# Three routed mixtures in a twelve-stage network: gate logits per tile, gather order, place sums, and statistics

## Chip, cores and metric

The kernel runs on one core of a Trainium2 chip. The metric is the device time of one execution in microseconds (us). The time before is 3292.99 us, the median of three runs (3290.18 to 3300.77).

## What is computed

`x` is a state of 1024 tokens by 256 values. Twelve blocks follow one another, each a residual over a layer norm: in each of four layers a cross attention, a self attention and a feed-forward block.

```python
x = x + L0_xattn(layernorm(x), ctx, ...)
x = x + L0_attn(layernorm(x), ...)
x = x + L0_ffn(layernorm(x), Wg, W1, W2, W3)
...                                   # L1: xattn, attn, ffn (a convolution)
x = x + L2_xattn(...); x = x + L2_attn(...)
x = x + L2_ffn(layernorm(x), wg_red, wg, w1, b1, w2, b2)
x = x + L3_xattn(...); x = x + L3_attn(...)
x = x + L3_ffn(layernorm(x), router_w, w1, w2)
```

Three feed-forward blocks are mixtures of 8 experts. Written per token they are:

```python
# L0_ffn: the two best of 8 experts, softmax over those two
logits = x @ Wg.T                       # 1024 x 8
out = sum over the two of  gate * ((silu(x @ W1[e].T) * (x @ W2[e].T)) @ W3[e].T)
# L2_ffn: the best expert; logits through a 16-wide reduction and unit rows
logits = (x @ wg_red.T) @ (wg / max(norm(wg), 1e-4)).T
out = max(softmax(logits)) * (gelu(x @ w1[e] + b1[e]) @ w2[e] + b2[e])
# L3_ffn: the two best; a token past an expert's capacity of 320 is dropped for it
out = sum over the two of  gate * keep * (gelu(x @ w1[e]) @ w2[e])
```

## The kernel before

All tokens live in `x`, 8 tiles of 128 tokens on the partitions by 256 values. `xn` holds the normalised rows in the same shape. The stages run one after another, as one program; within a stage a scheduler orders each engine's instructions by data, except where a helper pins an instruction to its place in the program's text (`pinned`, and everything while `self.fixed` is set). Each engine carries out its own list in order.

**The hand-over between stages.** When an attention has the output of a tile, `finish_x(t)` (L360) adds it to `x` on VectorE (DVE) and calls `ready(t)` (L294): statistics on DVE (bn_stats L300, bn_aggr L302), three tiny operations on GpSimd (POOL, L306 to L308: epsilon, power, product), and, one call later, `normalise` (L314) on ScalarE (ACT), which writes `xn`. The next stage transposes `xn` on TensorE (PE; `tr` is L200, `mm` L196) and copies it out of PSUM (`to_T`, `evac` L186 and L188). Where a layer has an output bias, `add_bias` (L353) adds it to all 8 tiles of `x` on POOL at some time after `xn` has been read from them.

**A mixture** (L0_ffn, L2_ffn, L3_ffn) has these steps:

1. `expert_rows`: `xn` is written to DRAM as `xin` (one DMA on the SP queue), with rows of zeros behind it; `xn` is transposed.
2. `gate_logits`: per tile two matmuls against the gate's 8 columns, all into one PSUM bank; one copy `lg` (L1417). In L2_ffn a reduction to 16 (`xr`) and the unit rows `wu` stand between (from L1653).
3. `top2` or `first_max` (L1382 and after): the best one or two experts per token as one-hot rows, on DVE. In `two_choices` the one-hots and gates are copied together (L1587 to L1591).
4. `places`: a matmul by ones gives the count per group of 128 tokens and expert; `cum` is their running sum over 16 groups (8 in L2_ffn), one dependent add of 8 columns each (L1431); `place` (L1435) adds the place within the group, from a triangular matmul.
5. `slots`: each token's slot in a list of tiles of 128 rows (23, 15 and 23 tiles for the three mixtures), `rows` (which expert's weights a tile needs), and by matmuls of `R` (L1495, a 128x128 compare for each group) with `V` (L1481 to L1488) the lists `token` and `share` (to L1505).
6. `experts`: for each tile, `fetch` brings the weights `W` (two DMAs on SP, L1522; 2.36 MB in L0_ffn, 2.10 MB in L2_ffn and L3_ffn; three buffers) at the row that SP reads out of `rows`, and gathers 128 rows of `xin` by `token` into `xs` (an indirect DMA on the POOL queue, L1524). `turn` transposes `xs`, `hidden` and the second matrix run on PE, `y` (L1554) is scaled by `share` and scatter-added to DRAM (L1555). Fetches go two tiles ahead:

```python
got = [fetch(0), fetch(1)]
xT = turn(got[0][1])
for i in range(tiles):
    W, xs = got.pop(0)
    if i + 2 < tiles:
        got.append(fetch(i + 2))
    hT = hidden(W, xT)
    if i + 1 < tiles:
        xT = turn(got[0][1])
```

Afterwards `x` is loaded back (four DMAs, L1561), and after L0_ffn and L2_ffn `ready(t)` runs for the 8 tiles.

**The stages around.** L0_attn ends in a loop over tiles (transposes of `att`, four `py` matmuls, `finish_x`) with a PSUM pool `pst` of two banks in its second part. L2_attn ends in two matmuls a tile over `oT`. L3_attn ends in an MLP, whose second matrix keeps PE busy up to the end; it begins with convolutions over `a` (copies L2026 out of transposed `xn`), and `kb` (L2014) is an operation of POOL at its start. L1_xattn follows L0_ffn, L3_xattn follows L2_ffn.

Of the kernel before, what the change touches and what calls it, by code (L numbers as in the profile page):

```python
# [16 lines left out]
P = 128  # L17
B, S, D = 16, 64, 256
NT = B * S // P
NTOK = B * S  # L20
# [154 lines left out]
class Net:  # L175
    def __init__(self, tc, io):
        self.tc, self.nc, self.io = tc, tc.nc, io
        self.flip = 0
        self.fixed = False
# [36 lines left out]
    def load_constants(self, pool):  # L216
# [24 lines left out]
        self.ident = self.c("ident")  # L241
        self.due = None
# [52 lines left out]
    def ready(self, t):  # L295


        nc, x = self.nc, self.x[:, t, :]
        st = self.stat.tile([P, 6], F32, tag="bst", name="bst")
        nc.vector.bn_stats(st, x)  # L300
        mv = self.stat.tile([P, 2], F32, tag="mv", name="mv")
        nc.vector.bn_aggr(mv, st)  # L302
        self.normalise()

        rs = self.stat.tile([P, 2], F32, tag="rs", name="rs")
        nc.gpsimd.tensor_tensor(rs[:, 0:1], mv[:, 1:2], self.c("eps"), ALU.add)  # L306
        nc.gpsimd.tensor_tensor(rs[:, 0:1], rs[:, 0:1], self.c("pow")[:, 0:1], ALU.pow)  # L307
        nc.gpsimd.tensor_scalar(rs[:, 1:2], mv[:, 0:1], rs[:, 0:1], -1.0, ALU.mult, ALU.mult)  # L308
        self.due = t, rs

# [39 lines left out]
    def add_bias(self, i):  # L350

        for t in range(NT):
            self.nc.gpsimd.tensor_tensor(self.x[:, t, :], self.x[:, t, :], self.bv(i), ALU.add)  # L353
# [225 lines left out]
    def L1_xattn(self, w):  # L579
# [8 lines left out]
        with (  # L588
# [4 lines left out]
            with (  # L593
                tc.tile_pool(name="l1xn", bufs=1) as wn,
                tc.tile_pool(name="l1xn_t", bufs=4, space=PSUM) as pst,
            ):
                xnT = self.norm_T(wn, pst, "pst")
                self.add_bias(2)
                for c in range(4):
                    for h in range(2):  # L600
                        ps = self.psum(pst, [P, 512], "pst")
                        tok = slice(h * 512, (h + 1) * 512)
                        self.project_T(ps, Wq, xnT, slice(c * P, (c + 1) * P), tok)
                        self.evac(qT[:, c, tok], ps)
            with (
# [123 lines left out]
                def at(t, fn, *args):  # L729
                    extra.setdefault(t, []).append((fn, args))  # L730

# [300 lines left out]
    def L0_attn(self, w):  # L1032
# [4 lines left out]
        with (  # L1037
# [78 lines left out]
            with (  # L1116
# [6 lines left out]
                state = {}  # L1123

# [196 lines left out]
    def L2_attn(self, w):  # L1321
        nc, tc = self.nc, self.tc
        Wq, Wk, Wv, Wfc = w
        with (
# [4 lines left out]
        ):  # L1329
            xnT = self.norm_T(wk, pst, "pst")  # L1330
# [46 lines left out]
    def first_max(self, small, lg, tag):  # L1377
# [3 lines left out]
        m = small.tile([P, NT, 1], F32, tag=f"m{tag}", name=f"m{tag}")  # L1381
        nc.vector.tensor_reduce(m, lg, AX.X, ALU.max)  # L1382
        oh = small.tile(shape, F32, tag=f"oh{tag}", name=f"oh{tag}")
# [5 lines left out]
        lo = small.tile([P, NT, 1], F32, tag=f"lo{tag}", name=f"lo{tag}")  # L1389
        nc.vector.tensor_reduce(lo, oh, AX.X, ALU.min)  # L1390
        nc.vector.tensor_tensor(oh, oh, lo.to_broadcast(shape), ALU.is_equal)
        return m, oh

    def top2(self, small, lg):

        nc = self.nc
        shape = [P, NT, E]
        m1, oh1 = self.first_max(small, lg, "a")
        lg2 = small.tile(shape, F32, tag="lg2", name="lg2")
        nc.vector.scalar_tensor_tensor(lg2, oh1, -BIG, lg, ALU.mult, ALU.add)  # L1400
        m2, oh2 = self.first_max(small, lg2, "b")
        e2 = small.tile([P, NT, 1], F32, tag="e2", name="e2")
        nc.vector.tensor_tensor(e2, m2, m1, ALU.subtract)
        nc.scalar.activation(e2, e2, AF.Exp)
        g1 = small.tile([P, NT, 1], F32, tag="g1", name="g1")
        nc.vector.tensor_scalar(g1, e2, 1.0, None, ALU.add)
        nc.vector.reciprocal(g1, g1)
        g2 = small.tile([P, NT, 1], F32, tag="g2", name="g2")
        nc.vector.tensor_tensor(g2, e2, g1, ALU.mult)
        return oh1, g1, oh2, g2  # L1410

    def gate_logits(self, small, pp, xT, w):
        ps = self.psum(pp, [P, NT, E], "pst")
        for t in range(NT):
            self.project_N(ps[:, t, :], xT, t, w)
        lg = small.tile([P, NT, E], F32, tag="lg", name="lg")
        self.nc.vector.tensor_copy(lg, ps)  # L1417
        return lg

    def places(self, small, pp, oh, K):  # L1420
# [3 lines left out]
        G = K * NT  # L1424
# [3 lines left out]
        cum = small.tile([P, G + 1, E], F32, tag="cum", name="cum")  # L1428
        nc.vector.memset(cum[:, 0, :], 0.0)
        for g in range(G):  # L1430
            nc.vector.tensor_tensor(cum[:, g + 1, :], cum[:, g, :], ps[:, g, :], ALU.add)  # L1431
        ps = self.psum(pp, [P, G, E], "pst")
        self.mm(ps.rearrange("p g e -> p (g e)"), self.c("tri"), flat)
        place = small.tile([P, G, E], F32, tag="place", name="place")
        nc.vector.tensor_tensor(place, ps, cum[:, :G, :], ALU.add)  # L1435
        return place, cum[:, NT, :], cum[:, G, :]

    def slots(self, small, pp, oh, gate, place, count, K, tiles):
# [54 lines left out]
        for g in range(G):  # L1493
            R = small.tile([P, P], F32, tag="R", name="R", bufs=3)
            nc.vector.tensor_scalar(R, self.c("iota128"), lo[:, g : g + 1], None, ALU.is_equal)  # L1495
            self.mm(ps, R, V[:, :, g, :], g == 0, g == G - 1)
# [11 lines left out]
    def experts(self, name, xin, slots, weights, width, cols, tiles, wp, sp, pst, pso, hidden):  # L1508
# [7 lines left out]
        def fetch(i):  # L1516
# [4 lines left out]
            for o in (slice(0, cols), slice(cols, width)):  # L1521
                nc.sync.dma_start(W[:, o], self.io[weights][bass.ds(r, P), o])  # L1522
            xs = sp.tile([P, D], F32, tag="xs", name="xs", bufs=3)
# [4 lines left out]
            return W, xs  # L1528
# [10 lines left out]
        got = [fetch(0), fetch(1)]  # L1539
        xT = turn(got[0][1])  # L1540
        for i in range(tiles):
            W, xs = got.pop(0)
            if i + 2 < tiles:
                got.append(fetch(i + 2))
            hT = hidden(W, xT)
            if i + 1 < tiles:
                xT = turn(got[0][1])
            n = hT.shape[1]
            W2 = W[:, cols : cols + n * D].rearrange("p (c n) -> p c n", n=D)
# [15 lines left out]
        if name != "l3":  # L1565
            for t in range(NT):
                self.ready(t)

    def expert_rows(self, wk, stat, pst, name):

        nc = self.nc
        xn = self.xn
        xin = self.dram.tile([NTOK + SPARE, D], F32, tag=f"{name}i", name=f"{name}i")
        nc.sync.dma_start(xin[:NTOK, :].rearrange("(t p) d -> p t d", p=P), xn)
        zero = wk.tile([P, D], F32, tag="zero", name="zero")
        nc.gpsimd.memset(zero, 0.0)
        nc.sync.dma_start(xin[NTOK:, :], zero)
        xnT = wk.tile([P, 2, NTOK], F32, tag="xnT", name="xnT")
        self.to_T(pst, "pst", xn, xnT)
        return xin, xnT  # L1580

    def two_choices(self, small, pst, oh1, g1, oh2, g2, cap=None):
# [3 lines left out]
        oh = small.tile([P, 2 * NT, E], F32, tag="oh", name="oh")  # L1586
        nc.vector.tensor_copy(oh[:, :NT, :], oh1)  # L1587
        nc.vector.tensor_copy(oh[:, NT:, :], oh2)
        gate = small.tile([P, 2 * NT], F32, tag="gate", name="gate")
        nc.vector.tensor_copy(gate[:, :NT], g1[:, :, 0])  # L1590
        nc.vector.tensor_copy(gate[:, NT:], g2[:, :, 0])  # L1591
# [14 lines left out]
    def L0_ffn(self, _):  # L1606
        nc, tc = self.nc, self.tc
        with (
# [8 lines left out]
            xin, xnT = self.expert_rows(wk, stat, pst, "l0")  # L1617
            lg = self.gate_logits(small, pst, xnT, self.gates[:, :, 0:E])
# [22 lines left out]
    def L2_ffn(self, _):  # L1641
        nc, tc = self.nc, self.tc
        shape = [P, NT, E]
        with (
# [8 lines left out]
            xin, xnT = self.expert_rows(wk, stat, pst, "l2")  # L1653

            sq = small.tile([E, 16], F32, tag="sq", name="sq")
            nc.vector.tensor_tensor(sq, self.wg2, self.wg2, ALU.mult)
            nr = small.tile([E, 1], F32, tag="nr", name="nr")
            nc.vector.tensor_reduce(nr, sq, AX.X, ALU.add)
            nc.gpsimd.tensor_tensor(nr, nr, self.c("pow")[:E, 1:2], ALU.pow)
            nc.vector.tensor_scalar(nr, nr, 1e-4, None, ALU.max)  # L1660
            nc.vector.reciprocal(nr, nr)
            wu = small.tile([E, 16], F32, tag="wu", name="wu")
            nc.vector.tensor_scalar(wu, self.wg2, nr, None, ALU.mult)
            ps = self.psum(pst, [P, E], "pst")
            self.tr(ps[:16, :], wu)
            wuT = small.tile([16, 1, E], F32, tag="wuT", name="wuT")
            nc.vector.tensor_copy(wuT[:, 0, :], ps[:16, :])
            xr = small.tile([16, 1, NTOK], F32, tag="xr", name="xr")
            for h in range(2):
                tok = slice(h * 512, (h + 1) * 512)  # L1670
                ps = self.psum(pst, [P, 512], "pst")
                self.project_T(ps[:16, :], self.gates[:, :, 2 * E : 2 * E + 16], xnT, slice(None), tok)
                nc.vector.tensor_copy(xr[:, 0, tok], ps[:16, :])
            lg = self.gate_logits(small, pst, xr, wuT)
            m, oh = self.first_max(small, lg, "a")
# [47 lines left out]
    def L3_ffn(self, _):  # L1723
        nc, tc = self.nc, self.tc
        with (
# [8 lines left out]
            xin, xnT = self.expert_rows(wk, stat, pst, "l3")  # L1734
            lg = self.gate_logits(small, pst, xnT, self.gates[:, :, E : 2 * E])
# [151 lines left out]
    def L3_attn(self, w):  # L1887
# [12 lines left out]
        with (  # L1900
# [10 lines left out]

            def turned(src, at):
# [157 lines left out]
            for u in range(NU):  # L2070
# [10 lines left out]
                z = sp.tile([P, 2, U], F32, tag="zk", name="zk")  # L2081
# [148 lines left out]
    def run(self, out, stages=STAGES):  # L2230
        tc = self.tc
        with (
# [15 lines left out]
            for i, name in enumerate(stages):  # L2248
                load(name)
                load(stages[i + 1] if i + 1 < len(stages) else None)  # L2250
# [26 lines left out]
```

## Time and profile before

| | |
|---|---|
| median of three runs | 3292.99 us (3290.18 to 3300.77) |
| the profiled execution's own time | 3295.64 us |
| its span (first to last instruction) | 3293.5 us |
| mean granted TensorE clock | 0.946 |
| matmuls (PE) busy | 3032.2 us, 92% |
| VectorE, ScalarE, GpSimd busy | 1292.8, 1322.4, 376.2 us |
| L0_ffn: last sum of the attention / first expert tile / reload of x | 615.49 / 655.95 / 851.22 |
| L2_ffn: last xn / first expert tile / reload of x | 2459.42 / 2490.15 / 2607.92 |
| L3_ffn: last xn / first expert tile / reload of x | 3077.30 / 3110.57 / 3284.16 |

Lines of the timeline read: start in us, duration in us of the group, engine, line of the kernel, operation, written tile <- read tiles, shape, number of instructions, and in brackets how long the engine stood idle before and what ended that. In the list of waits each line gives the waiting engine, its tile and line, what released it, and the total, the number and the longest of the waits. In the table by stretches, columns are the window, its length, the busy time (and number) of PE, PE's weight load, DVE, ACT and POOL, then the granted clock of PE, the share in which the 16 DMA engines were busy, and GB/s.

### The profile page before, as it was taken

Reading aid. Unit: us, or ns where it says so; the run is one execution under the profiler, and the core shown is the slowest. Engines: PE = TensorE matmul, PEld = TensorE weight load, DVE = VectorE, ACT = ScalarE, POOL = GpSimd, SP = SyncE. Lnnn points to the kernel's source line nnn. Section 1 sums busy time; section 2 is a strip of 40 time slices with the busy share of each in tenths; the row PEclk is TensorE's granted clock in tenths of the full one; section 3 lists DMA queues with packets and bytes.
Section 4 is the critical chain, followed back from the end, with each engine's and each line's share of the span. In section 5 each row is a group of like instructions: output and inputs, shape, how many; then the busy total and the mean of one; then the engine's idle time right before and its main releaser. Section 6 shows DMA issues by size and latency. Waiting matters only on the chain. (4 is left out here: it accounts for less than half of the span.)

```text
span 3293.5 us, 67180 instructions
## 1 busy us (share of the span) xinstructions
PE 3032.2 (92%) x28455; PEld 2256.3 (69%) x28455; DVE 1292.8 (39%) x3454; ACT 1322.4 (40%) x2640; POOL 376.2 (11%) x538
## 2 busy tenths in 40 slices
PE   7999997699799999999997899999979788899798
PEld 5666664599566666666665677777748676778697
DVE  6888884422244444444447721221242100045300
ACT  5888884211233333333331122222222377753111
POOL 0000002233200000000001100000012311111132
PEclk9999997699899999999997899999988899988799
DMA  6334430389111121121266011111208555510397
GB/s 219 108 122 134 134 118 31 135 289 319 48 60 61 60 81 60 61 76 45 80 212 208 13 41 60 61 40 60 76 17 298 160 175 189 182 47 1 142 326 247
DMA packets 178360, 395.06 MB, mean 120 GB/s; under 512 B 11446, under 2 KB 142270, under 8 KB 165214
## 3 DMA queue, kind: packets, MB, share of 16 engines
q1 hardware_dynamic: 165070, 372.91, 32.9%
q0 software_dynamic: 11712, 16.00, 2.3%
q8 instruction: 224, 3.67, 0.5%
q10 hardware_dynamic: 1280, 1.87, 0.2%
q14 instruction: 74, 0.61, 0.1%
HBM read 375.02 MB, written 16.12 MB: 119 GB/s over the span
## 5 line engine op out<-in xcount | busy, mean ns | idle before, releaser
L196 PE MATMUL acc<-ctx,st 128*128 128x257 f32 (+1 forms) x1664 | 397.2, 383 | 0.0
L196 PE MATMUL pss<-qk,ctxT 128*128 128x512 f32 (+1 forms) x832 | 388.8, 592 | 0.6 <-DVE qk L631 0.6
L196 PEld LDWEIGHTS acc<-ctx,st 128*128 128x128 f32 (+1 forms) x1664 | 310.2, 190 | 95.1 <-issue 35.4
L456 DVE CUSTOM_DVE_ANT_0 Sx<-s,mneg 128x384 f32<-128x384 f32 (+1 forms) x512 | 264.2, 570 | 88.3 <-PE s L196 88.3
L647 DVE TENSOR_TENSOR top<-pss,top 128x512 f32<-128x512 f32 x192 | 132.6, 691 | 407.4 <-ACT st L642 407.3
L200 PE MATMUL pst<-cst,Sx 128*128 128x128 f32 (+1 forms) x1736 | 254.9, 286 | 25.1 <-ACT Sx L1358 10.5
L671 ACT ACTIVATE st<-st 128x512 f32<-128x512 f32 (+1 forms) x208 | 130.6, 629 | 290.5 <-DVE st L670 290.5
L930 ACT ACTIVATE Pr<-pss 128x512 f32<-128x512 f32 (+1 forms) x512 | 219.8, 524 | 62.8 <-PE pss L196 61.6
L500 ACT ACTIVATE PT<-pst 128x384 f32<-128x384 f32 x512 | 215.1, 489 | 63.2 <-PE pst L200 62.1
L200 PEld LDWEIGHTS pst<-cst,Sx 128*128 128x128 f32 (+1 forms) x1736 | 188.2, 142 | 72.7 <-ACT PT L500 27.5
L196 PEld LDWEIGHTS pss<-qk,ctxT 128*128 128x128 f32 (+1 forms) x832 | 154.1, 186 | 120.6 <-issue 102.7
L642 ACT COPY st<-pss 128x512 f32<-128x512 f32 (+1 forms) x208 | 121.6, 585 | 205.0 <-PE pss L196 205.0
L196 PE MATMUL pso<-W,hT 128*128 128x256 f32 x884 | 200.9, 379 | 0.0
L196 PE MATMUL pst<-wst,ctxT 128*128 128x256 f32 (+1 forms) x832 | 183.4, 380 | 0.0
L196 PE MATMUL psk<-ctxT,wst 128*128 128x512 f32 (+1 forms) x512 | 181.8, 513 | 0.8 <-ACT qT L792 0.8
L196 PEld LDWEIGHTS pso<-W,hT 128*128 128x128 f32 x884 | 163.2, 190 | 19.7
L196 PEld LDWEIGHTS pst<-wst,ctxT 128*128 128x128 f32 (+1 forms) x832 | 153.5, 186 | 25.9 <-issue 2.7
L196 PE MATMUL pss<-q,ctxT 32*128 32x128 f32 (+1 forms) x3328 | 149.4, 297 | 17.0 <-issue 14.1
L832 DVE TENSOR_TENSOR v<-pst,bvec 128x512 f32<-128x512 f32 (+1 forms) x112 | 73.1, 652 | 204.5 <-PE pst L196 204.5
L353 POOL TENSOR_TENSOR x<-x,bvec 128x256 f32<-128x256 f32 x40 | 29.9, 749 | 1079.1 <-ACT xn L314 1079.1
L196 PEld LDWEIGHTS psk<-ctxT,wst 128*128 128x128 f32 x512 | 88.3, 190 | 93.7 <-issue 92.1
L196 PEld LDWEIGHTS pss<-q,ctxT 32*128 32x128 f32 (+1 forms) x3328 | 118.4, 192 | 47.6 <-issue 35.9
(400 smaller groups left out, 4502.3 us busy)
## 6 DMA issues: line engine op xcount, KB each, us to landing
ctxT<-in_ctxT_dram SPq DMA_DIRECT2D x64, 1601.0 KB
W<-in_L_experts_dram SPq DMA_DIRECT2D x61, 1024.0 KB
ctx<-in_ctx_dram SPq DMA_DIRECT2D x32, 1536.0 KB
W<-in_L_experts_dram SPq DMA_DIRECT2D x23, 1536.0 KB
ctx<-in_ctx_ones_dram SPq DMA_DIRECT2D x16, 1632.0 KB
ctx<-in_ctx_one_dram SPq DMA_DIRECT2D x16, 1542.0 KB
W<-in_L_experts_dram SPq DMA_DIRECT2D x23, 768.0 KB
W<-in_L_experts_dram SPq DMA_DIRECT2D x15, 1028.0 KB
```

What stands on the lines that cost most here:

```text
L196: self.pinned(self.nc.tensor.matmul(out, lhsT, rhs, start=start, stop=stop))
L200: self.pinned(self.nc.tensor.transpose(out, in_, self.ident[:n, :n]))
L353: self.nc.gpsimd.tensor_tensor(self.x[:, t, :], self.x[:, t, :], self.bv(i), ALU.add)
L456: self.pinned(nc.vector.tensor_tensor_reduce(out=Sx[:, j, :n], in0=ps[j][:, :n], in1=st["mneg"][:, o : o + n], op0=ALU.add, op1=ALU.max, s ...
L500: self.pinned(nc.scalar.activation(PT, ps, AF.Exp))
L642: pin(nc.scalar.copy(st[:kn], ps[:kn]))
L647: pin(nc.vector.tensor_tensor(top[b][:kn], ps[:kn], top[b][:kn], ALU.max))
L671: pin(nc.scalar.activation(st, st, AF.Exp, scale=HD**-0.5))
L832: nc.vector.tensor_tensor(o, ps[:kn, :n, :], bv[:kn].to_broadcast([kn, n, D]), ALU.add)
L930: nc.scalar.activation(st["Pr"][:kn, g : g + n, j, :], ps[j][:kn, :n, :], AF.Silu)
```

## The change

Five things are changed.

- **Gate logits by tiles in the preceding attention.** Before an attention that is followed by a mixture, `open_gate` makes `xin` and writes its zero rows (and for L2 the unit rows `wu`). `ready(t)` of that attention then calls `gate_step(t - 2)`: the gate matmuls of tile k-1 and their copy into `lg`, then the DMA of `xn[k]` to `xin`, two transposes of it, and an ACT copy `gx` (one buffer). `close_gate`, at the mixture's start, does the steps that are left. `expert_rows` and `gate_logits` go.
- **Shorter sums.** `places` sums in log steps (1, 2, 4, 8) over all columns at once; `top2` writes its one-hots and gates straight into the joint tiles; `slots` compares four groups at a time.
- **Gathers first.** The first two gathers are issued ahead of the second expert's weights. For that, SP reads the later weights' rows out of `rest`, a copy of `rows` made on POOL behind those two gathers.
- **Statistics by four tiles.** After L0_ffn and L2_ffn, `ready_all` replaces the 8 calls of `ready`: statistics of all tiles, a power of four columns for each half, and `xn` in turns on ACT and DVE.
- **add_bias pinned**, with L1_xattn's call moved from its start into step 3 of its loop. In L3_attn the tag `zk` becomes `z`.

With the changed program's lists beside those before, the 8 `add_bias` adds form one block on POOL in L0_attn, L1_xattn and L1_attn; in L3_attn POOL's list is `kb`, five adds, and then the last tile's three operations with one add after each. Between output matmuls of L2_attn, the matmuls of a tile stand behind the gate step of a tile three to four earlier.

```diff
@@ ready
         self.normalise()
+        if self.gate is not None:
+            self.gate_step(t - 2)
...
+    def ready_all(self):
+        nc, pin = self.nc, self.pinned
+        self.fixed = True
+        parts = []
+        for h in range(2):
+            mv = self.stat.tile([P, 4, 2], F32, tag="mv4", name="mv4", bufs=2)
+            for i in range(4):
+                st = self.stat.tile([P, 6], F32, tag="bst", name="bst")
+                pin(nc.vector.bn_stats(st, self.x[:, 4 * h + i, :]))
+                pin(nc.vector.bn_aggr(mv[:, i, :], st))
+            rs = self.stat.tile([P, 2, 4], F32, tag="rs4", name="rs4", bufs=2)
+            pin(nc.vector.tensor_scalar(rs[:, 0], mv[:, :, 1], 1e-5, None, ALU.add))
+            nc.gpsimd.tensor_tensor(
+                rs[:, 0], rs[:, 0], self.c("pow")[:, 0:1].to_broadcast([P, 4]), ALU.pow
+            )
+            parts.append((mv, rs))
...
@@ places
-        for g in range(G):
-            nc.vector.tensor_tensor(cum[:, g + 1, :], cum[:, g, :], ps[:, g, :], ALU.add)
+        nc.vector.tensor_copy(cum[0][:, pad:, :], ps)
+        step = 1
+        while step < G:
+            nc.vector.tensor_tensor(
+                cum[1][:, pad:, :], cum[0][:, pad:, :], cum[0][:, pad - step : pad - step + G, :],
+                ALU.add,
+            )
+            cum.reverse()
+            step *= 2
@@ slots
-        for g in range(G):
-            R = small.tile([P, P], F32, tag="R", name="R", bufs=3)
-            nc.vector.tensor_scalar(R, self.c("iota128"), lo[:, g : g + 1], None, ALU.is_equal)
-            self.mm(ps, R, V[:, :, g, :], g == 0, g == G - 1)
+        for g in range(0, G, 4):
+            R = small.tile([P, 4, P], F32, tag="R", name="R", bufs=2)
+            nc.vector.tensor_tensor(
+                R, self.c("iota128").unsqueeze(1).to_broadcast([P, 4, P]),
+                lo[:, g : g + 4].unsqueeze(2).to_broadcast([P, 4, P]), ALU.is_equal,
+            )
+            for i in range(4):
+                self.mm(ps, R[:, i, :], V[:, :, g + i, :], g + i == 0, g + i == G - 1)
@@ experts
-        got = [fetch(0), fetch(1)]
-        xT = turn(got[0][1])
+        W, xs = {0: fetch(0, rows)}, [gather(0), gather(1)]
+        rest = sp.tile([P, tiles], U32, tag="rest", name="rest", bufs=1)
+        self.pinned(nc.gpsimd.tensor_copy(rest, rows))
+        W[1] = fetch(1, rest)
+        xT = turn(xs.pop(0))
         for i in range(tiles):
-            W, xs = got.pop(0)
             if i + 2 < tiles:
-                got.append(fetch(i + 2))
+                W[i + 2] = fetch(i + 2, rest)
+                xs.append(gather(i + 2))
...
         if name != "l3":
-            for t in range(NT):
-                self.ready(t)
+            self.ready_all()
@@ gate_step
+        if 0 <= k - 1 < NT:
+            xT = g["xT"].pop(k - 1)
+            ps = self.bank()
...
+                for kc in range(2):
+                    self.mm(
+                        ps[:, 0, :E], xT[:, kc, :], self.gates[:, kc, o : o + E], kc == 0, kc == 1
+                    )
+            pin(nc.vector.tensor_copy(g["lg"][:, k - 1, :], ps[:, 0, :E]))
+        if k < NT:
+            nc.sync.dma_start(g["xin"][k * P : (k + 1) * P, :], self.xn[:, k, :])
+            ps = self.bank()
+            for kc in range(2):
+                self.tr(ps[:, kc, :], self.xn[:, k, kc * P : (kc + 1) * P])
+            xT = g["xT"][k] = self.gpool.tile([P, 2, P], F32, tag="gx", name="gx", bufs=1)
+            pin(nc.scalar.copy(xT, ps[:, :2, :]))
@@ add_bias
-            self.nc.gpsimd.tensor_tensor(self.x[:, t, :], self.x[:, t, :], self.bv(i), ALU.add)
+            self.pinned(self.nc.gpsimd.tensor_tensor(
+                self.x[:, t, :], self.x[:, t, :], self.bv(i), ALU.add
+            ))
@@ L1_xattn
-                self.add_bias(2)
...
+                at(3, self.add_bias, 2)
@@ run
+                after = stages[i + 1] if i + 1 < len(stages) else None
+                load(after)
+                if name[3:] == "attn" and after in ("L0_ffn", "L2_ffn", "L3_ffn"):
+                    self.open_gate(after[:2].lower())
```

## Prediction

> **What bounds the kernel now.** I read the page's busy shares first, then the list of what TensorE (PE) waited for, then the timeline around the three mixtures, and last the table by stretches, for clock and DMA.
>
> ```profile
> PE 3032.2 (92%) x28455; PEld 2256.3 (69%) x28455; DVE 1292.8 (39%) x3454; ACT 1322.4 (40%) x2640; POOL 376.2 (11%) x538
> ```
>
> The waits (us in total, times, longest):
>
> ```profile
> PE pst L200 <- ACT xn L314: 64.5, 31, 16.9
> PE pst L196 <- POOL V L1485: 21.4, 3, 8.2
> ...
> PE pst L200 <- DMA xs<-l0i,token: 8.0, 1, 8.0
> PE pst L200 <- DMA xs<-l3i,token: 7.2, 1, 7.2
> ...
> PE pst L196 <- DVE oh L1588: 3.5, 1, 3.5
> ```
>
> PE is busy 92% of the span; the change cannot touch that bulk. What it touches are the places where PE stands still: between an attention and a mixture's first expert (the V, xs and oh rows), and at the entry of a stage, where PE waits for normalised rows (the xn row). Each has one chain to walk, so I price chains. The largest, L0_ffn's, from the last tile's sum to the first expert:
>
> ```profile
> 615.49 0.42 DVE L360 TENSOR_TENSOR x<-py,x 128x256 f32<-128x256 f32 x1 [1.11 <-PE py L196]
> ...
> 620.24 7.00 PE L196 MATMUL pst<-gates,xnT 128*128 128x8 f32 x32 [0.46 <-ACT xnT L186]
> 627.28 0.22 DVE L1417 COPY lg<-pst 128x64 f32<-128x64 f32 x1 [6.77 <-PE pst L196]
> ...
> 631.50 3.10 DVE L1431 TENSOR_TENSOR cum<-cum,pst 128x8 f32<-128x8 f32 x16 [0.66 <-PE pst L196]
> ...
> 647.88 1.30 POOL L1524 DMA_INDIRECT xs<-l0i,token  x1 [8.17 <-DVE share L1505]
> ...
> 654.82 0.66 PE L200 MATMUL pst<-cst,xs 128*128 128x128 f32 x2 [7.96 <-DMA xs<-l0i,token]
> ```
>
> The gate matmuls take 7.00 us, the 16 dependent sums 3.10, and from the first gather's issue to the rows' use pass 6.94. The table by stretches tells what the gather stands behind (columns: busy time and count of the five engines, granted clock, DMA share, GB/s):
>
> ```profile
> 647.50:655.90 8.40, 0.66 (x2) 0.29 (x2) 0.16 (x2) 0.37 (x1) 3.49 (x4) 0.50 0.99 411
> ...
> 680.00:700.00 20.00, 20.00 (x148) 19.07 (x148) 4.57 (x10) 2.33 (x5) 6.32 (x5) 1.00 0.94 324
> ```
>
> While PE waits, DMA runs full with the second and third expert's weights; its clock is 0.50. In the loop PE is busy 20.00 of 20.00, so nothing is won there.
>
> **1. Gate logits by tiles.** One step is a pair of transposes (0.27 us at full clock: L3_ffn's row of 8 took 1.09), an ACT copy (about 0.37, from the 0.37 that ACT is busy with the first xT), four gate records (0.48: 3.89 us for 32) and a DVE copy of 8 columns (0.16, by L1431's single adds). Most steps lie inside the attention; steps 7 and 8, and part of 6, stay behind the last xn.
>
> L0: from the last sum (615.49) to the end of the logits' copy (627.50) is 12.0 now. After: that sum comes 2.0 later (six steps of 0.75 are 4.5; the eight transposes that already stand there and their stalls, 2.5, go), 3.55 from it to xn7 as now (619.04), and 3.3 for the remainder at the clock of 0.50: 8.85. **Saves 3.2**; 0 if the two PSUM banks of this pool make PE wait for DVE at each step, 5 if PE's idle time there takes the steps for nothing.
> L2: from xn7's end (2459.42) to the logits (2468.45) is 9.03. After, xn7 comes 1.2 later (output matmuls now stand behind the chain of xn three to four tiles earlier; POOL paces that chain at 1.13 a tile), and the rest, with one more copy, is 4.0. **Saves 3.8** (2.3 to 5.3).
> L3: there the second FC matrix fills PE up to 3074.12; five pairs and four gates ahead of its end cost 5 x 0.27 + 4 x 0.48 = 3.3. The remainder is 2.7 in place of 5.2 (3077.30 to 3082.51). **Loses 0.8** (from 3 lost to 1 gained).
>
> **2. Shorter sums.** 16 adds of 8 columns (3.10) become a copy and four adds of 128 columns. L1435, of that size, took 0.28; with the hop about 0.32 each, 1.6. The oh copy ahead of the ones matmul (0.25) goes. Four 128x512 compares replace 16 of 0.28; nothing is won, since PE's 7.10 us over V bound that part, but the first one is longer (0.69 by the 128x512 row of L647), about 0.3 lost. L0 1.35, L3 0.95 (other DVE work is spread between its adds), L2 0.7 (half as many sums): **3.0** (1.5 to 4).
>
> **3. First rows ahead of the second weights.** SP now issues all three experts' weights (7.1 MB) as soon as rows is known (638.18), so the first gather at 647.88 finds a full queue. After, only the first expert's 2.36 MB are ahead, 5.7 us at 411 GB/s, gone by then. Bounds for issue to use: with no stream, the scatter before 851.22 landed 2.3 after its end, plus 1.1 of issue: 3.4; in the loop, with one expert under way, the page's median is 4.5. I take 3.4, as the queue is empty. L0 6.94 - 3.4 = 3.5 (2.4 at 4.5), L3 6.24 - 3.4 = 2.8 (1.7). L2 nothing: its b2 matmuls hold PE until 2488.95, 7.8 after the gather's issue. **6.3** (4.1 to 6.5).
> The price is a later W[1]: two gathers (1.30 + 1.04 + 0.3), the copy of rows on POOL and the register load (1.2 from rows to issue now) put it 4.3 behind the first gather; at 411 GB/s it is whole at 10 to 12, at the loop's 324 GB/s at 13.6. Its use is at 14.5 (3.4, then 1.1 to the first expert, then its 8.4 at half clock and output). Covered, by 1 to 4; below that each us late is a us lost. In L3 the tile is shorter, and the cover is 0.3 to 3.
> [...]
>
> **4. Statistics by four.** After L0_ffn the tiles pass one at a time through POOL, with add_bias (0.72 each) in between; the first bn starts at 853.99, the last xn ends at 867.41:
>
> ```profile
> 863.23 0.72 POOL L353 TENSOR_TENSOR x<-x,bvec 128x256 f32<-128x256 f32 x1
> ...
> 866.81 0.60 ACT L314 ACTIVATE xn<-x,rs 128x256 f32<-128x256 f32 x1 [1.09 <-POOL rs L308]
> ```
>
> After: eight pairs of bn (0.42 + 0.17 with hops, 5.7), a 128x4 power (about 1.0), a product, then four xn split between ACT and DVE (1.2): 8.4 instead of 13.4. The transposes and copies then come in a heap, so I count 3.0 of the 5 (2.5 to 4). After L2_ffn 10.3 (2610.72 to 2621.05) becomes 8.4: 1.9. **4.9** (4 to 6).
>
> **5. add_bias pinned.** POOL now gets its eight adds as one block. In L0_attn, L1_xattn and L1_attn it stands behind the last statistics: nothing. At the start of L3_attn it does not:
>
> ```profile
> 2917.88 0.40 POOL L2014 TENSOR_SCALAR kb<-bvec 128x256 f32<-128x256 f32 x1 [5.00 <-PE acc L200]
> ...
> 2919.55 0.69 POOL L307 TENSOR_TENSOR rs<-rs,cst 128x1 f32<-128x1 f32 x1
> 2920.34 0.27 POOL L308 TENSOR_SCALAR rs<-mv,rs 128x1 f32<-128x1 f32 x1
> 2920.64 0.60 ACT L314 ACTIVATE xn<-x,rs 128x256 f32<-128x256 f32 x1 [8.58 <-POOL rs L308]
> 2921.15 2.02 ACT L2026 COPY a<-ps 128x512 f32<-128x512 f32 x4
> ```
>
> In the changed order POOL does kb (waiting for pool memory until 2917.88), five adds (3.65), and then the three operations of the last tile's rs with two adds among them: 2918.28 + 3.65 + 0.33 + 0.73 + 0.69 + 0.73 + 0.27 = 2924.7, xn at 2925.3 in place of 2921.24. All four copies to a are behind that xn on ACT, and the convolutions (PE, DVE) behind them. **Loses 4.1**; 0 if the block gets done ahead of kb's wait.
>
> The eight writes of xin on SP, one for each tile, stand ahead of nothing due before rows; zero rows and their copies move to the start, where SP runs ahead: nothing. The joint z/zk buffer in L3_attn: 0 (to 1 lost).
>
> **Sum.** 3.2 + 3.8 - 0.8 + 3.0 + 6.3 + 4.9 - 4.1 = 16.3. The profiled execution took 3295.64 (span 3293.5), so it would take 3279.3. The median shown is 3292.99, 2.65 less; from it the forecast is **3276.7, say 3277**.
>
> **Rivals.**
> *The attention gives it all back*: steps inside L0_attn and L2_attn delay the last xn by as much as they shorten the tail (DVE copies of logits behind sums and bn, two banks). Part 1's gains of 7.0 gone: 3284. For it: the bank count; against: PE waits 1 us or more per tile in L0's tail now.
> *The gather's time is its own*, not the queue's: part 3's 6.3 gone, 3283. For it: the loop's 4.5, over the scatter's 3.4 with half the load only 1.1 more; against: 6.94 and 6.24 behind a full queue. [...]
> *POOL's block at L3_attn is hidden* (adds done ahead of kb): 3273. Against: kb stands first in the order.
> *Slower*: the xn chain becomes the beat of the output loop. From a sum to its xn is 3.55, and a step's copies and matmuls make it 4.8. With an output matmul behind the step of the tile n earlier, a tile takes at least 4.8/n. L0's tiles come each 2.3 to 3.2 now, L2's each 1.13; the order gives n of 3 to 4 in L2, hence my 1.2. Should held banks or the single gx buffer make n one, L2 loses 7 x 3.7 = 26 and L0 7 x 2 = 14: 3314. It decides from n under 1.5 on.
>
> **Chances.** Forecast 0.60 (own range 3270 to 3284), given back 0.12, gather's own 0.08, POOL hidden 0.14, slower 0.06. Range 3265 to 3289: it takes in the ends of parts 1 to 5 as far as they would fall together, and four of the rivals' cases. A measurement of this kernel can tell about 0.3% (10 us) from no change: under 3283 faster, 0.75; same 0.19; slower 0.06.
>
> **What would show it.** Gather to first transposes 3.4 in L0_ffn and L3_ffn, with W[1] landing before the second expert's first matmul and no PE gap there; single adds of 0.28 in places; from the first bn to the last xn 8.4 after L0_ffn; at L3_attn's start xn at 4 us behind the last statistics, behind five adds. It is wrong if PE's output loops in L0_attn or L2_attn stretch by more than 4 us, if L3_ffn loses over 3 by its steps, or if experts wait for weights.

## The result, and the profile after

The changed kernel takes 3283.99 us (median of 20 runs, 3272.93 to 3296.03) against 3293.20 (20 runs, 3282.37 to 3306.43). The ratio is 0.9969, with a 95% interval of 0.9956 to 0.9982: faster by 6 to 14 us. The forecast was 3277, with a range of 3265 to 3289. The profiled execution has a span of 3288.2 us, 5.3 less than the one before; single executions of either kernel lie up to 13 us off their medians, so what follows compares stretches inside the traces, and times only where several runs stand behind them.

The page's busy shares (the changed kernel):

```profile
PE 3033.4 (92%) x28479; PEld 2261.1 (69%) x28479; DVE 1293.5 (39%) x3430; ACT 1322.4 (40%) x2650; POOL 364.3 (11%) x495
```

PE's work is the same to about 1 us (3032.2 before). What changed is the waiting. The list of PE's waits (total, times, longest):

```profile
PE pst L201 <- ACT xn L345: 28.8, 2, 15.7
...
PE pst L201 <- DMA m<-in_mask_dram: 16.0, 1, 16.0
PE pst L201 <- ACT xn L353: 15.5, 9, 4.9
...
PE pst L201 <- ACT gx L1682: 5.6, 5, 3.5
...
PE pst L197 <- ACT gx L1682: 5.2, 7, 1.4
...
PE pst L201 <- DMA xs<-l0i,token: 4.3, 1, 4.3
...
PE pst L201 <- DMA xs<-l3i,token: 4.1, 1, 4.1
```

The waits for the gathered rows are 4.3 and 4.1 in place of 8.0 and 7.2. New are 10.8 us of waiting for `gx`, the ACT copy of a gate step, and a wait of 4.9 for `xn` at the start of L3_attn (its line is shown with the block of bias adds). The line of 64.5 for `xn` before seems to have shrunk to 28.8 + 15.5, but this is no gain of that size: the program's very first wait (16.9 before) was put down to `xn` there and is put down to the mask's DMA here (16.0). With it and the 4.9 the waits are 65.2.

The same stretches in both profiled executions (ends read from their timelines; "saved" is positive):

| stretch | before | after | saved | forecast |
|---|---|---|---|---|
| L0_attn, first sum to last logits copy | 44.7 | 46.8 | -2.1 | 3.2 |
| L2_attn, first sum to last logits copy | 20.2 | 24.8 | -4.6 | 3.8 |
| L3_attn, first MLP sum to last logits copy | 45.9 | 46.3 | -0.4 | -0.8 |
| logits to first gather, L0 / L2 / L3 | 20.4 / 12.7 / 20.7 | 19.2 / 12.4 / 19.5 | 2.6 | 3.0 |
| first gather to its use, L0 / L2 / L3 | 6.94 / 7.83 / 6.24 | 3.25 / 8.08 / 3.12 | 6.6 | 6.3 |
| reload of x to L1_xattn's first sum | 178.3 | 171.9 | 6.4 | 3.0 |
| reload of x to L3_xattn's first sum | 60.7 | 58.1 | 2.6 | 1.9 |
| L3_attn, last sum before it to its second projections | 47.0 | 53.1 | -6.1 | -4.1 |

The sum is 5.0, close to the 5.3 by which the two spans differ. The stretches differ in how far one pair of executions can be trusted. Over all the profiled kernels that share the changed kernel's statistics, the one up to L1_xattn takes 171.5 to 176.0; those of L0 and L2 are compared over more kernels below.

L0's chain after the change, from the timeline:

```profile
603.52 1.94 PE L201 MATMUL pst<-cst,Sx 128*128 128x128 f32 x8 [3.49 <-ACT gx L1682]
...
617.89 0.44 PE L201 MATMUL pst<-cst,att 128*128 128x128 f32 x2 [0.52 <-ACT gx L1682]
...
623.65 0.42 DVE L401 TENSOR_TENSOR x<-py,x 128x256 f32<-128x256 f32 x1 [1.94 <-PE py L197]
...
634.48 1.27 DVE L1474 TENSOR_TENSOR cum<-cum 128x128 f32<-128x128 f32 x4
...
649.63 1.30 POOL L1577 DMA_INDIRECT xs<-l0i,token  x1 [8.44 <-DVE share L1555]
...
652.88 0.66 PE L201 MATMUL pst<-cst,xs 128*128 128x128 f32 x2 [4.26 <-DMA xs<-l0i,token]
```

The four sums take 1.27 and the gather's rows are used 3.25 after its issue, as forecast. But the attention's last sum comes at 623.65, 8.2 later than before (615.49), not 2.0. Counted from the attention's first sum it is 7.3, and 2.2 of these belong to one tile, the first with a step: PE waits 3.49 us for `gx`, where the kernel before waited 1.37 for `xn`, and in the 5 us behind that the clock is 0.51 (1.00 before). The tiles after it take 5.08, 4.52, 3.69 and 3.16 where they took 3.17, 3.16, 2.34 and 2.28.

### The profile page after: what moved, and what is told of

It is laid out like the page before. It is cut to its first block, busy times and chain, and to the rows that moved or that the text cites. A ratio compares the mean times of both kernels' runs of the same rounds, so it can differ in the third digit from the quotient of the medians.

```text
span 3288.2 us, 67222 instructions
## 1 busy us (share of the span) xinstructions
PE 3033.4 (92%) x28479; PEld 2261.1 (69%) x28479; DVE 1293.5 (39%) x3430; ACT 1322.4 (40%) x2650; POOL 364.3 (11%) x495
## 3 DMA queue, kind: packets, MB, share of 16 engines
q8 instruction: 225, 3.69, 0.5%
## 5 line engine op out<-in xcount | busy, mean ns | idle before, releaser
L516 ACT ACTIVATE Sx<-Sx,neg 128x384 f32<-128x384 f32 (+1 forms) x256 | 145.7, 620 | 11.5 <-DVE neg L507 11.4
```

The source lines that it names most:

```text
L516: self.pinned(nc.scalar.activation(Sj[j], Sj[j], AF.Identity, bias=st["neg"][:, j - 2 : j - 1]))
```

## Experiments

All kernels below start from the changed kernel, unless it is said otherwise. Ratios are to the kernel before, with 95% intervals; where there is no ratio, there is a single execution, and it is read by its stretches.

### The gate steps

**Undone in all three mixtures.** `expert_rows` and `gate_logits` are taken back from the kernel before; the rest of the change stays.

```diff
-            xin, lg = self.close_gate("l0", small, pst)
+            xin, xnT = self.expert_rows(wk, stat, pst, "l0")
+            lg = self.gate_logits(small, pst, xnT, self.gates[:, :, 0:E])
```

> The changed kernel with its gate logits as before, in one batch behind each attention; sums, gathers, statistics and pinned bias stay. Theory: the steps inside the attentions cost more PE time than they hide (by the trace of the changed kernel L0 loses 2.1, L2 4.6, L3 0.4 us from the attention's sums to the last logits), so this runs about 7 us below the changed kernel, 16 below the kernel before, and the last sum of L0_attn and of L2_attn comes back by 7 and 10 us. Rival, the prediction's own terms: the steps save 6 us and something else took the gain; then this is 6 us above the changed kernel.

3275.28, ratio 0.9954 (0.9936 to 0.9973), 9 below the changed kernel's median. L0 passes from the first sum to the logits in 43.0 (46.8 with the steps), L2 in 20.8 (24.8); counted from the first sum, the last sums come back by 7.7 and 10.3, as expected. The two ratios' intervals overlap. In L2 the stretches do not: over all the profiled kernels here it takes 20.2 to 21.9 with the logits in a batch and 22.5 to 24.9 with the changed kernel's steps; in L0 it is 43.0 to 45.5 and 45.5 to 54.0. In L3 no difference shows (45.8 to 48.8 and 45.9 to 46.6). The rival (6 above) falls. A second pair of kernels on record, both with L3_attn's bias adds free, says the same of the whole: 3281.18 with the steps, 3269.97 with the batch.

**One PSUM bank for a step.**

```diff
+        bank = self.bank()
         if 0 <= k - 1 < NT:
             xT = g["xT"].pop(k - 1)
-            ps = self.bank()
+            ps = bank[:, 2:]
...
-            ps = self.bank()
+            ps = bank
             for kc in range(2):
                 self.tr(ps[:, kc, :], self.xn[:, k, kc * P : (kc + 1) * P])
```

> The changed kernel with logits and transposes of one gate step in one PSUM bank in place of two. Theory: in L0_attn the transposes of att wait 0.52 us a tile for the copy of the gate step, because the pool has two banks; with one bank less in use that wait goes and the tail of L0_attn is 3 to 4 us shorter, while L2_attn, which is full of PE work, stays as it is: 3.5 us below the changed kernel. Rival: the wait is for ACT's order or the stretch is PE's work alone; then the last sum of L0_attn moves by less than 1 us.

3308.83, ratio 1.0047 (1.0029 to 1.0064): slower, against both. Its timeline in L0_attn:

```profile
615.71 0.44 PE L201 MATMUL pst<-cst,xn 128*128 128x128 f32 x2 [0.97 <-DVE lg L1676]
...
615.98 0.38 PE L201 MATMUL pst<-cst,att 128*128 128x128 f32 x2
```

The wait of `att` is gone, as the theory said, but the transposes of `xn` now wait for the logits' copy out of the same bank (0.97), which stands on DVE behind the tile's sum and statistics. L0's stretch is 52.6, L2's 38.1. In this trace PE does not write one part of the bank while DVE has yet to read another: in two successive tiles the copies `lg` end at 615.65 and 620.30, and the transposes start at 615.71 and 620.36. What would follow if they started earlier, no run shows. So the bank wait is real, 0.52 of a tile's growth of 1.36 (period 4.52 against 3.16), and the rest, 0.84, is the step's own matmuls.

**L2: what sets the tile.** First the two gate matrices multiplied together once, ahead of the loop, so that a step needs four gate records and no copy `xr`:

```diff
             if g["name"] == "l2":
-                w = self.gates[:, :, 2 * E : 2 * E + 16]
                 for kc in range(2):
-                    self.mm(ps[:16, 1, :], w[:, kc, :], xT[:, kc, :], kc == 0, kc == 1)
-                xr = self.gpool.tile([16, P], F32, tag="xr", name="xr", bufs=1)
-                pin(nc.vector.tensor_copy(xr, ps[:16, 1, :]))
-                self.mm(ps[:, 0, :E], xr, g["wuT"])
+                    self.mm(ps[:, 0, :E], xT[:, kc, :], g["M"][:, kc, :], kc == 0, kc == 1)
```

> The changed kernel with L2's two gate matrices multiplied together once (256 x 8), so that a gate step of L2_attn has four gate records in place of six and one copy less. Theory: in L2_attn's tail the steps cost PE time, since PE is full there (2.29 us a tile, of which the output matmuls are 0.9); with 0.5 us less PE work in a step a tile takes about 1.8, and from the first sum to the last logits pass about 20 us in place of 24.8. Rival: the tile is set by the chain through xn and the copies; then it stays above 2.1.

Then the steps four tiles behind instead of two (`gate_step(t - 4)` in L2_attn):

> The changed kernel with L2_attn's gate steps two tiles further behind (four tiles in place of two). Theory (PE is full): the tiles between sums that have a step take 2.2 to 2.4 us as now; only fewer of them stand before the last sum, and from the first sum to the last logits pass 24 to 26 us as in the changed kernel (24.8). Rival (the prediction's slower case, the chain through xn is the beat): with two tiles more of slack the tiles take 1.4 or less, and the last logits come 4 us or more earlier.

With the product, L2 takes 18.9 from the first sum to the logits and a tile 1.8 on average (2442.67 to 2449.75 for four). With the longer lag a tile with a step still takes 1.9 to 2.3. The last sum comes 6.5 earlier, as fewer steps stand ahead of it, but four are left behind it at 3.13 each (clock 0.51 there), and the whole is 25.4. So inside the loop it is PE's work that sets the tile and not the chain through `xn`. The changed kernel's timeline of one tile there:

```profile
2446.49 0.61 PE L197 MATMUL pst<-gx,gates 128*16 128x128 f32 x4
...
2447.04 0.44 PE L201 MATMUL pst<-cst,xn 128*128 128x128 f32 x2
...
2447.31 0.60 PE L197 MATMUL pst<-wst,oT 128*128 128x256 f32 x2
...
2447.84 0.38 PE L197 MATMUL pst<-wuT,xr 16*128 16x8 f32 x2
...
2448.15 0.70 PE L197 MATMUL pst<-wst,oT 128*128 128x256 f32 x2
...
2448.78 0.61 PE L197 MATMUL pst<-gx,gates 128*16 128x128 f32 x4
```

Each group starts where the one before it is through: no PE wait in the 2.29 us from gate to gate. And the table by stretches of the kernel before says that there was nothing to fill:

```profile
2445.00:2453.00 8.00, 8.00 (x37) 7.03 (x36) 6.15 (x19) 1.21 (x3) 2.97 (x10) 0.88 0.00 0
```

PE was busy 8.00 of 8.00, with output matmuls and six transposes that feed them, at a clock of 0.88. One more loss stands ahead of the loop. The changed kernel's PE is idle 2.19 us for the first `xn`, and the four output matmuls behind that take 1.91 at a clock of 0.50; with the longer lag this wait is 0.46 and the four take 1.03.

### The block of bias adds

**Free again in L3_attn.**

```diff
+            self.fixed, was = False, self.fixed
             self.add_bias(8)
+            self.fixed = was
```

> The changed kernel with the eight bias adds of L3_attn free to move again, so that they stand between the statistics of L3_xattn. Theory: the block cost a wait of 4.0 us and, since PE stood idle for 4.9 us there, the clock of the convolutions behind it (5.27 us for twelve matmuls against 2.83): L3_attn's start comes back by 6.1, the twelve matmuls take 2.8 again, and the whole is 6 us below the changed kernel. Rival: only the wait counts, 4 us, and the matmuls' 5.27 has another cause and stays.

**In the block, with PE kept busy.** 34 transposes that nobody reads stand before the ones that wait; that is work added.

```diff
             for u in range(NU):
+                if u == NU - 1:
+                    idle = bank()
+                    for _ in range(34):
+                        self.tr(idle[:, 0, :P], self.xn[:, 0, :P])
                 ps = bank()
```

> The changed kernel with 34 transposes of a tile that nobody reads (extra work, some 4.4 us at full clock) put before the transposes that wait for the last xn at the start of L3_attn. Theory: the block of bias adds costs that stage twice, by the wait and by the clock that falls in it; with PE busy the twelve matmuls behind the wait take 2.8 in place of 5.27 and the stage loses some 4 us against the kernel before in place of 6.1. Rival: the matmuls are slow for another reason, the adds or copies beside them; then they stay above 4.5.

The three timelines, first the changed kernel's:

```profile
2910.28 3.46 POOL L392 TENSOR_TENSOR x<-x,bvec 128x256 f32<-128x256 f32 x5
...
2916.08 0.60 ACT L353 ACTIVATE xn<-x,rs 128x256 f32<-128x256 f32 x1 [10.23 <-POOL rs L313]
...
2916.73 0.90 PE L201 MATMUL ps<-cst,xn 128*128 128x128 f32 x3 [4.93 <-ACT xn L353]
...
2917.43 5.27 PE L197 MATMUL ps<-a,dgs 128*128 128x256 f32 x12
```

With the adds free:

```profile
2913.16 0.55 PE L201 MATMUL ps<-cst,xn 128*128 128x128 f32 x3 [1.44 <-ACT xn L353]
...
2913.63 2.83 PE L197 MATMUL ps<-a,dgs 128*128 128x256 f32 x12
```

With the block and the idle transposes (47 in the first line are 13 and 34):

```profile
2903.06 5.35 PE L201 MATMUL ps<-cst,xn 128*128 128x128 f32 x47 [0.52 <-DVE x L401]
...
2909.66 0.55 PE L201 MATMUL ps<-cst,xn 128*128 128x128 f32 x3 [1.25 <-ACT xn L353]
...
2910.13 2.83 PE L197 MATMUL ps<-a,dgs 128*128 128x256 f32 x12
```

From the last sum to the first projections pass 18.3 before, 24.5 after, 18.3 with free adds, 21.6 with the block and a busy PE. So a busy PE gives back 2.9 us, although the block stands as it did: that part is the clock, which is low behind PE's idle 4.93 us (granted 0.53 from 2917 to 2923, against 1.00 from 2922 to 2928 before). The other 3.4 us are the wait. In each of the other runs with the block these twelve matmuls took 4.3 to 5.2, in each without it 2.8. Free adds give 3281.18, ratio 0.9963 (0.9941 to 0.9985), 2.8 below the changed kernel's median where 6 were expected; the times do not tell the two apart, the stretch does. Behind the wait of 4.93 us the twelve matmuls took 5.27 us; behind the 1.44 us with free adds they took 2.83, the time that they took in the kernel before at a clock of 1.00. How long a wait must be for the clock to fall, these two do not show, and a shorter one than 4.93 us had a fall behind it too: 2.19 us in the changed kernel, ahead of output matmuls of L2_attn, with a clock of 1.00 from 2438.00 to 2439.10 and of 0.50 from 2441.46 to 2443.40. In the kernel before 0.50 stood behind a wait of 2.97 us there (up to 2443.96), but the clock was at 0.55 in 2440 to 2441 already, ahead of it.

### The gathers

Two kernels put all three weights ahead of the gathers again, with a further copy of 2.36 (2.10) MB behind them.

```diff
-        W, xs = {0: fetch(0, rows)}, [gather(0), gather(1)]
...
+        W = {i: fetch(i, rows) for i in range(3)}
+        junk = self.dram.tile([P, width], F32, tag=f"{name}j", name=f"{name}j")
+        nc.sync.dma_start(junk, self.io[weights][0:P, :])
+        xs = [gather(0), gather(1)]
```

> The changed kernel with all three weights issued ahead of the first gathers, as before, and behind them one more copy of 2.36 (2.10) MB from DRAM to DRAM, whose data nobody uses. Theory: the gather stands behind what SP has issued; it then lands 5.5 us or more later than in the kernel before, 12 us after its issue in L0_ffn and 11 in L3_ffn. Rival: the DMA engines take turns between queues; then a deeper queue changes nothing, and the gather lands 6 to 7 us after its issue, as before. The extra copy may delay later weights; only the first gather is read.

In this run the scheduler moved the extra copy to the program's start, so it only undoes the gather's part: 7.47 us from issue to use in L0, 6.88 in L3, in place of 3.25 and 3.12. The second takes the copy's row out of `rows`, which holds it at its place:

> The changed kernel with all three weights issued at rows, as before, and behind them, now held at that place, one more copy of 2.36 (2.10) MB from DRAM to DRAM that nobody uses. If the gather stands behind all that SP has issued, it is used 12 us after its issue in L0_ffn, 11 in L3_ffn. If the gather's packets only start some us late under load and then run beside the weights', as the queues' packets by microsecond suggest for the kernel before, it is used after 6.5 to 8.5 us, hardly later than the 6.94 and 6.24 of before.

7.40 and 6.88, against 6.94 and 6.24 before: with a third more in the queue the gather is 0.5 and 0.6 us later, not about 5 us, as it would be if it stood behind all of it. The DMA view by queue (packets, MB, share of 16 engines; q1 is SP's, q0 POOL's) shows how. Before the change, 3 to 5 us after the gather's issue, and 5 to 7 us:

```profile
q1 hardware_dynamic: 87, 0.81, 95.6%
q0 software_dynamic: 14, 0.06, 7.0%
```

```profile
q1 hardware_dynamic: 55, 0.68, 82.8%
q0 software_dynamic: 55, 0.16, 20.1%
```

With the deeper queue, 5.0 to 7.4 us after the issue, and after the change, 2.0 to 3.0 us:

```profile
q1 hardware_dynamic: 81, 0.76, 78.8%
q0 software_dynamic: 78, 0.23, 23.9%
```

```profile
q0 software_dynamic: 48, 0.13, 42.5%
```

The gather does not stand behind the weights: its packets run beside theirs, while in the last case but one over 1.6 MB of weights and extra copy are still to come. But under load the first packet moves some 4 us after the issue in place of 2, and then the gather has a fifth to a quarter of the engines' time in these windows, in place of 42.5%. That the load is what costs holds; that the queue's length does, which is how the prediction put it, falls. Why the first packet starts later under load stays open.

### The statistics

**Tile by tile again** (`ready` for each tile in place of `ready_all`; the bias adds of L1_xattn stay late).

> The changed kernel with the statistics after L0_ffn and L2_ffn tile by tile, as before; the bias adds of L1_xattn stay late. Theory: at L1_xattn most of the gain (4.8 us from the first statistics to the projections) came from the bias adds leaving POOL's chain, 3 to 3.5, and 1.5 from the batch; at L3_xattn, where no bias stands in that chain, all 2.6 came from the batch. So from the reload of x to L1_xattn's first sum the kernel loses 1 to 2 us against the changed one, to L3_xattn's 2 to 3. Rival: the batch of four is what counts; then 4 to 5 are lost at L1_xattn.

From the reload to L1_xattn's first sum it takes 174.8, to L3_xattn's 62.0, where the changed kernel took 171.9 and 58.1. Neither decides: kernels with the changed kernel's statistics take 171.5 to 176.0 and 57.7 to 62.5. The stretch from the first statistics to the last `xn` is short enough to be read from single traces:

| first statistics to last `xn`, us | before | tile by tile, bias adds late | changed |
|---|---|---|---|
| after L0_ffn | 13.43 | 10.27 | 8.50 |
| after L2_ffn | 10.32 | 10.32 | 7.34 |

So of the 4.9 us won at L1_xattn, 3.2 come from the bias adds leaving POOL's chain and 1.8 from the batch, close to what was expected; at L3_xattn, where no bias stood in that chain, all 3.0 are the batch's. The rival (4 to 5 us by the batch at L1_xattn) falls by this stretch. What of it reaches the whole program's time, this single execution can't tell.

### Parts put together

All with shorter sums, gathers first, statistics by four, and L3_attn's adds free. Gate logits in a batch:

> Both of the first two edits: gate logits in a batch as before, and L3_attn's bias adds free. Theory: the two do not touch, 7 + 6 us below the changed kernel, that is 22 below the kernel before (0.993). Rival (the prediction's terms): 4 below the sum of +6, so about 2 us above the changed kernel.

The same, with L2's gate matrices multiplied together once:

> Shorter sums, gathers first, statistics by four, L3_attn's bias adds free, gate logits in a batch behind the attention as before, and L2's two gate matrices multiplied together once. Theory: as the run with batch logits and free bias (3270, 23 below the kernel before), and L2's logits come about 3 us earlier, since 4.81 + 1.95 us of matmuls become some 3.9: 3267, a ratio of 0.992. Rival: the product's own chain (two transposes, two matmuls, three copies) comes to stand on the path and takes the 3 us back: 3270.

As the first, but L2's logits by tiles with the product:

> Shorter sums, gathers first, statistics by four, L3_attn's bias adds free; gate logits of L0 and L3 in a batch as before, those of L2 by tiles inside L2_attn with the two matrices multiplied together once. Theory: what each part gave alone adds up. Against the run with all three in a batch and free bias (3270), L2 passes from the first sum to the last logits in 18.8 in place of 21.9, so 3267, a ratio to the kernel before of 0.992 (0.990 to 0.994). Rival: the parts that were read from single profiles were the scatter between executions; then it is 3270 to 3275.

| | median, us | ratio to before |
|---|---|---|
| changed kernel | 3283.99 | 0.9969 (0.9956 to 0.9982) |
| batch logits, free adds | 3269.97 | 0.9931 (0.9910 to 0.9951) |
| the same with L2's product | 3271.46 | 0.9945 (0.9925 to 0.9965) |
| L2 by tiles with the product | 3270.66 | 0.9942 (0.9928 to 0.9956) |

All three are faster than the kernel before. Against the changed kernel, only the first one's interval lies wholly below; the medians of the other two are 12.5 and 13.3 us lower, but their intervals touch the changed kernel's or overlap it. Between the three the runs do not decide. The first came out as expected (0.993). The two kernels with the product were both expected at 3267 and came out at 3271.46 and 3270.66, close to where their rivals had put them. In a batch the product gains 1 us (21.9 to 20.9 in L2) and not 3: its 32 gate records of 8 columns take 6.93 us, about what as many took in L0_ffn of the kernel before (7.00 us at a clock of 0.50). By tiles it gains 3 (18.9), which the totals do not resolve.

## Why the prediction was right, and where not

The direction and the range held; the forecast of 16 us was nearly double the 9 measured, and the time came out at the rival "the attention gives it all back" (3284). That the time lies in the range rests partly on luck: the gate logits cost 7.1 us where 6.2 were to be won, and the statistics, larger than forecast in this pair of executions, made up for some of it.

- **Gate logits by tiles, +6.2 forecast, -7.1 measured.** This is the step that failed. "That sum comes 2.0 later" in L0 was 7.3, and "xn7 comes 1.2 later" in L2 was 8.3, both counted from the attention's first sum. In L0 the step's matmuls were priced nearly rightly (0.75; 0.84 measured). But only six were counted, and 2.5 us were taken off for eight transposes that already stood there and for their stalls; the stall did not go, PE waits 3.49 us for `gx` where it waited 1.37 for `xn`, with a clock of 0.51 behind it in place of 1.00. The bank wait of 0.52 per tile was left to the range. In L2 the error is larger: the tile's beat was taken from POOL's chain (1.13), and PE's own load was never looked up. It was full (8.00 of 8.00 us). There the step's 1.4 us (a tile's 2.29 less 0.9 for the output matmuls) came on top. The rival's mechanism for the loss (sums and copies on DVE) was not the main one.
- **L3's steps, -0.8 forecast, -0.4 measured**: there PE was seen to be full, and every record was counted. The same reading in L2 would have given the right sign.
- **Sums, 3.0 and 2.6; gathers, 6.3 and 6.6**: right in size. W[1] was never late: PE has no gap before the second expert, whose first matmuls start at 664.91 in L0_ffn and 3114.68 in L3_ffn, as the first expert's last ones end. The gather's mechanism was told wrong (above).
- **Statistics, 4.9 and 9.0**: mis-sized, though the 9.0 are those of one pair. The last `xn` came 4.9 earlier at L1_xattn, where the prediction had 5.0 and counted 3.0 for "a heap" of transposes, and 3.0 earlier at L3_xattn, where it counted 1.9. The first projections follow the first statistics 4.8 earlier at L1_xattn (9.34 after, 14.17 before), so the heap took nothing back there. What the stretch of 6.4 has beyond that lies within its scatter (171.5 to 176.0).
- **Block of adds, -4.1 and -6.1**: the order and the wait were right (the last `xn` 3.6 us later behind the last sum), the clock behind the wait was not in the sum.
- The "slower" rival had the chain through `xn` as the beat. The longer lag excludes it for L2.

The forecast's terms with the measured sizes add to 5 us. Between that and the 9 of the medians lies the scatter of single executions, some of which is seen below; what part of it is this pair's cannot be told.

## What to carry to other kernels

Before work is moved under another stage, read the busy time of the engine that will do it in that very stretch; a pace set elsewhere is no sign of room. A wait on PE can have a second price in the matmuls behind it: after 4.93 us of waiting twelve of them took 5.27 us instead of 2.83. So price such a wait with the clock that the profile grants behind it; these traces give no length below which it is safe. When an order is pinned, look at each place where the pinned helper is used: no wait of PE is put down to the bias adds in four of the attentions, and in the fifth they cost 6 us.

## What was not expected of the hardware

- The middle of L3_attn, which no kernel here edits, takes 45.7 to 52.3 us between its second projections and its MLP, by whether PE gets its full clock there: granted 0.52 over 17 us in both profiled executions of the comparison, 0.87 over 12.4 us in that of the batch kernel with the product, for the same matmuls. L3_xattn varies from 241.8 to 249.6. This is larger than most of the change's terms.
- DVE's five `dgs` operations took 2.91 us beside POOL's adds in the changed kernel and 2.94 with PE kept busy, 1.04 in the kernel before and with free adds, where no add stands beside them. What slows them there, no run separates.
